# Seeding PSUM with stored products: a recurrence cut into 512 runs of 32 tokens instead of 256 runs of 64

## The chip, the cores and the metric

The kernel runs on one core of a Trainium2 chip. The metric is the device time of one execution in microseconds. Before the change it is 7006.53 us, the median of 3 runs (7005.77 to 7007.88). Engines are called as in the profile: PE is TensorE, with PEld its weight loads, DVE is VectorE, ACT is ScalarE, POOL is GpSimd, and SP issues most of the DMAs.

## What is computed

Four images of 128 channels and 64x64 = 4096 tokens go through a convolution-style attention, a multi-head attention with feed-forward, and at last a recurrent layer. Only the last layer's arithmetic is changed:

```python
def _L1_ffn_ref(x, W, V, gamma, beta):
    Wx = jnp.einsum('bti,hi->bth', x, W)
    flat = Wx.reshape(B * T, H)
    mean = jnp.mean(flat, axis=0)
    var = jnp.var(flat, axis=0)
    Wx = ((flat - mean) * jax.lax.rsqrt(var + BN_EPS) * gamma + beta).reshape(B, T, H)
    def step(yt, wx_t):
        yt = jax.nn.sigmoid(wx_t + yt @ Vt)
        return (yt, yt)
    _, ys = jax.lax.scan(step, y0, jnp.swapaxes(Wx, 0, 1))
...
t = t + _L1_ffn_ref(_ln_t(t), L1_ffn_W, L1_ffn_V, L1_ffn_gamma, L1_ffn_beta)
```

So each token's 128 features are multiplied by W, normalised per feature over all 4x4096 tokens, and then fed one token after another into y = sigmoid(wx + V y), for 4 images side by side. V is orthogonal. The result is added to the token stream. All numbers are fp32.

## The kernel before, in words

**Stages.** Each image goes through a first stage (`first_stage`: the convolution attention of this image, with the feed-forward of the image before it spread in between, lines 1349 to 1395) and a second stage (`second_stage`: its multi-head attention). The last image's feed-forward has a stage of its own (`third_stage`, line 1435). Then come a short stage "fold", the stage "runs" with the recurrence, and the output. A conditional block at the end (line 1602) computes everything again in a slow, sequential way if a check of the result fails.

**Feed-forward.** `feed_forward` (line 1116) is a generator that handles one block of 512 tokens; each `yield` ends a step. In a first stage up to three generators are active and their steps are called from inside the convolution attention (`in_steps`, `meanwhile`), in an order written out by hand for PE, ACT and DVE. In the third stage eight generators run, one started per step, and the framework orders the instructions. At its end a block's normalised tokens are transposed by PE into PSUM (line 1245). `last` (line 1306) then copies them with ACT into SBUF, at once in the order that the recurrence wants (`"p (t c) -> p c t"`, line 1313): for images 0 to 2 into a buffer that SP stores to DRAM (line 1317), for image 3 into `every`. Two steps later `token_products` (line 1252) multiplies them by W on PE into PSUM, and DVE's `bn_stats` (line 1256) reads the product for the statistics; the product itself is thrown away. `hold_every` (line 1459) sets up the tile `every`, 128 channels x 4 images x 4096 tokens, has ACT's queue load images 0 to 2 from DRAM, and GpSimd's queue load W.

**Fold.** `fold_norm` (line 1260) gathers the statistics into `scale` and `shift` per feature, with a power on GpSimd (line 241), scales the rows of W with `scale`, transposes the result on PE and copies it into `WsT`. The normalisation is then W's scaled product plus `shift`.

**Recurrence.** With `C, L = 64, S // 64` (line 1300) an image's 4096 tokens are cut into 64 runs of 64 tokens; all 256 runs of the four images advance together. Every run but an image's first begins with 16 warm-up steps over the last tokens of the run before it (`WARM`, line 1504), so that its state has forgotten where it began. The runs are held in two streams of two images, 128 columns each (`NS`, line 1512). Per step and stream PE does a product with `WsT` of the next step's tokens (`begin`, line 1536, line 1539), a product with V on top of it in PSUM (line 1560), and ACT a sigmoid with `shift` as its bias (line 1567), which overwrites the token in `every`. PE's and ACT's order is written out by hand. There are 16+64 = 80 steps.

**Output.** Sixteen tiles `t2s` of 128 x 1024 hold the stream t2 that the result is added to; SP loads them at the start of the stage (line 1519). After steps 15, 31, 47 and 59 DVE adds the finished tokens of all sixteen tiles (`add_tokens`, line 1543); the last four tokens are added after the loop, tile by tile, with each tile's output DMA behind it, on SP's and ACT's queues in turn (lines 1593 to 1596). DVE also compares each run's end with the warm-up's end of the next run (lines 1580 to 1591); this sets the flag `bad_int` for the conditional block.

Of the kernel before, what the change touches and what calls it, by code (L numbers as in the profile page):

```python
# [10 lines left out]
F32 = mybir.dt.float32  # L11
# [15 lines left out]
def kernel(  # L27
# [32 lines left out]
    P = 128  # L60
# [61 lines left out]
    def half_tile(name):  # L122
        return get("half", name)
# [4 lines left out]
    def one_psum(name):  # L128
        return get("ps_one", name)
# [983 lines left out]
            mirrored(room, *by)  # L1113
        return late[1::2]

    def feed_forward(im, i, t2_rows, last, final):


        n, cols = im["n"], ts(i, IC)
# [123 lines left out]
        yield  # L1243
        yield
        pt = transposed(blocks(u), f"pl{n}_{i}")
        tokens_i = last(n, i, pt)
        yield
        yield
        if n != "r":
            token_products(n, i, tokens_i)  # L1250

    def token_products(n, i, tokens):

        pw = one_psum(f"pwx{n}_{i}")
        nc.tensor.matmul(pw, WT_sb, tokens, start=True, stop=True)
        nc.vector.bn_stats(wx_stats[:, n * NIC + i, :], pw)

    shift = const.tile([P, 1], F32, tag="shift", name="shift")

    def fold_norm(W_sb, WsT):  # L1260

        bmv = once.tile([P, 2], F32, tag="bmv", name="bmv")
        nc.vector.bn_aggr(bmv, wx_stats)
        scale = once.tile([P, 1], F32, tag="scale", name="scale")
        nc.vector.tensor_tensor(scale, rsqrt(bmv[:, 1:2], 1e-5, [P, 1], "bn"), gamma_sb, ALU.mult)
        nc.vector.tensor_tensor(shift, bmv[:, 0:1], scale, ALU.mult)
        nc.vector.tensor_tensor(shift, beta_sb, shift, ALU.subtract)
        Ws = half_tile("Ws")[:, 0:P]
        nc.vector.tensor_scalar(Ws, W_sb, scale, None, ALU.mult)
        pw = one_psum("pws")  # L1270
        nc.tensor.transpose(pw[:, 0:P], Ws, ident)
        nc.vector.tensor_copy(WsT, pw[:, 0:P])
# [24 lines left out]
        }  # L1297


    C, L = 64, S // 64  # L1300

    def feed_forwards(im, final=False):

        n, rows = im["n"], im["rows"]

        def last(n, i, pt):
            cols = ts(i, IC)
            dst = held["every"][:, n, cols] if final else get("fhalf", f"last{n}_{i}")
            if n == "r":
                nc.scalar.copy(dst, pt)  # L1310
            else:

                nc.scalar.copy(
                    dst.rearrange("p (t c) -> p c t", t=L), pt.rearrange("p (c t) -> p c t", t=L)
                )
            if not final:
                nc.sync.dma_start(out=last_dram[rows, cols], in_=dst)
            return dst


        order = [(i + 2 * NTG // NQB) % NTG for i in range(NTG)]
        return [feed_forward(im, i, t2_dram[rows, :], last, final) for i in order]

    def step_first(queue):

# [133 lines left out]
    def hold_every():  # L1459

        pool = ends.enter_context(tc.tile_pool(name="every", bufs=1))
        held["every"] = pool.tile([P, N, S], F32, tag="every", name="every")
        for name in ("W", "WsT"):
            held[name] = pool.tile([P, P], F32, tag=name, name=f"{name}_sb")
        nc.gpsimd.dma_start(out=held["W"], in_=W)
        for n in range(N - 1):
            for i in range(2):
                cols = ts(i, S // 2)
                nc.scalar.dma_start(out=held["every"][:, n, cols], in_=last_dram[ts(n, P), cols])
# [24 lines left out]
    before["close"]()  # L1494


    with stage("fold", half=(HALF, 1), ps_one=(ONE, 1)):
        fold_norm(held["W"], held["WsT"])

    WARM, TOL = 16, 1e-6
    LEAST, MOST = 1e-25, 1e25
    every = held["every"]

    by_run = every.rearrange("p n (i t c) -> p n i t c", t=L, c=IC // L)
# [5 lines left out]
    with stage("runs", t2=((P, 2 * IC), 4 * N), half=(HALF, 2 * NS + 2), ps_one=(ONE, 2 * NS)):  # L1514
# [12 lines left out]
        def tokens_at(k, t):  # L1527
            return by_run[:, ts(k, NN), :, t % L, :]

        def chunks(ap):  # L1530
            return ap.rearrange("p n (i c) -> p n i c", c=IC // L)


        wx = {}

        def begin(k, t):
            wx[k] = one_psum(f"wx{k}_{t + WARM}")[:, 0 : NN * C]
            out_k = wx[k].rearrange("p (n i c) -> p n i c", n=NN, c=IC // L)
            nc.tensor.matmul(
                out_k, held["WsT"], tokens_at(k, t), start=True, stop=t == -WARM, skip_group_check=True  # L1540
            )

        def add_tokens(t0, t1):

            for n, i, t2 in t2s:
                at = t2.rearrange("p (i c t) -> p i t c", i=2, t=L)[:, :, t0:t1]
                nc.vector.tensor_tensor(at, at, by_run[:, n, ts(i, 2), t0:t1], ALU.add)  # L1547


        marks = [0, 16, 32, 48, L - 4, L]  # L1550
        added = {t1: (t0, t1) for t0, t1 in zip(marks, marks[1:-1])}
        with tc.manual_schedule(engines={nc.tensor.engine, nc.scalar.engine}):
            y = [None] * NS
            for k in range(NS):
                begin(k, -WARM)
            for t in range(-WARM, L):
                for k in range(NS):
                    acc = wx[k].rearrange("p (n i c) -> p n i c", n=NN, c=IC // L)
                    if y[k] is not None:
                        nc.tensor.matmul(  # L1560
                            acc, VT_sb, y[k], start=False, stop=True, skip_group_check=True
                        )
                    if t + 1 < L:
                        begin(k, t + 1)
                    w = warm[2 * k + t % 2]
                    y[k] = chunks(w[:, :, 1:]) if t < 0 else tokens_at(k, t)
                    nc.scalar.activation(y[k], acc, AF.Sigmoid, bias=shift)
                    if t == -1:
                        y[k] = chunks(w[:, :, 0:C])
                if t + 1 in added:  # L1570
                    add_tokens(*added[t + 1])
        in_range = small.tile([P, 1], F32, tag="in_range", name="in_range")
        good = half_tile("good")[:, 0 : N * NT]
        inv = inverses.rearrange("p i k -> p (i k)")
        nc.vector.tensor_scalar(good, inv, LEAST, None, ALU.is_ge)
        nc.vector.scalar_tensor_tensor(good, inv, MOST, good, ALU.is_le, ALU.mult)
        nc.vector.tensor_reduce(in_range, good, AX.X, ALU.min)
        ok = half_tile("ok")[:, 0 : N * C].rearrange("p (n c) -> p n c", n=N)
        for k in range(NS):
            nc.vector.tensor_tensor(  # L1580
                chunks(ok[:, ts(k, NN), :]), y[k], chunks(warm[2 * k + 1][:, :, 1:]), ALU.subtract
            )
        nc.vector.tensor_tensor(ok, ok, ok, ALU.mult)
        nc.vector.tensor_scalar(ok, ok, TOL * TOL, None, ALU.is_le)
        nc.vector.tensor_reduce(least, ok, AX.XY, ALU.min)
        nc.vector.tensor_tensor(least, least, in_range, ALU.mult)
        pl = one_psum("pleast")
        nc.tensor.transpose(pl[0:1, 0:P], least, ident)
        nc.vector.tensor_reduce(bad[:, 0:1], pl[0:1, 0:P], AX.X, ALU.min)
        nc.vector.tensor_scalar(bad[:, 1:2], bad[:, 0:1], -1.0, 1.0, ALU.mult, ALU.add)  # L1590
        nc.vector.tensor_copy(bad_int, bad[:, 1:2])

        add_tokens(L - 4, L)
        for n, i, t2 in t2s:
            eng = nc.sync if i % 2 == 0 else nc.scalar
            eng.dma_start(out=out[n][:, ts(i, 2 * IC)], in_=t2)

    ends.close()
    state = const.tile([P, N], F32, tag="state", name="state")
# [2 lines left out]
    with tc.If(any_bad > 0):  # L1602
# [5 lines left out]
        with stage(  # L1608
# [3 lines left out]
            for n in range(N):  # L1612
                nc.sync.dma_start(out=every[:, n, :], in_=last_dram[ts(n, P), :])
                for i in range(NIC):
                    token_products(n, i, every[:, n, ts(i, IC)])
# [96 lines left out]
```

## Time and profile before

| what | us |
|---|---|
| median of 3 runs | 7006.53 |
| the profiled execution's own time | 7005.9 |
| its span, first to last instruction | 7004.2 |
| inside it: `shift` ready / first output DMA issued | 6896.03 / 6978.31 |
| PE busy over the span | 6828.0 (97%) |
| DVE busy over the span | 5934.9 (85%) |
| ACT busy over the span | 5960.0 (85%) |
| POOL busy over the span | 2772.7 (40%) |

The profile is one execution. Its stretches are read by a table of busy times, its single instructions by the timeline: start, length, engine, line, operation, output tile, input tiles, partitions x elements, and how many equal instructions in a row the row stands for; in brackets stands how long the engine was idle ahead of it, and on what it waited. A row of several instructions overlaps with rows of other engines. Groups of instructions give busy time and mean length, and after the second bar the idle time of the engine just before them. Matmul ends are modelled. In the timeline a product in fp32 appears as two passes, each with its own weight load.

### The profile page before, as it was taken

How to read it: one execution, taken by the hardware profiler on the slowest of the kernel's cores; microseconds unless marked ns; L12 is line 12 of the kernel's file. 1: busy time of each engine (PE TensorE's matmuls, PEld its weight loads, DVE VectorE, ACT ScalarE, POOL GpSimd, SP SyncE). 2: the span in 40 equal slices, each digit the busy share in tenths (PEclk: the TensorE clock that was granted, in tenths of full speed). 3: DMA queues.
4: the chain of work that ended last, by engine and by line, in shares of the span. 5: the costliest groups of instructions: out<-in, count | busy, mean ns of one | idle time of the engine just before them, and what ended most of it. 6: DMA issues, size and time to landing. Idle time of an engine off the chain costs nothing. (4 is left out here: it accounts for less than half of the span.)

```text
span 7004.2 us, 224421 instructions
## 1 busy us (share of the span) xinstructions
PE 6828.0 (97%) x92782; PEld 3702.0 (53%) x92782; DVE 5934.9 (85%) x8086; ACT 5960.0 (85%) x11927; POOL 2772.7 (40%) x9893
## 2 busy tenths in 40 slices
PE   8999999999999999999999999999999999999987
PEld 4545555555664555555565555555466555555546
DVE  6688889887888989898787898988878888889884
ACT  4479999996669999999566999999856799999986
POOL 1134444434343444343433443444343444444431
PEclk9999999999999999999999999999999999999998
DMA  1110000000111000000011100000011100000012
GB/s 31 37 41 25 24 27 21 22 10 23 50 54 39 24 21 21 21 21 20 24 47 49 38 21 22 21 25 22 19 31 45 57 22 21 25 29 22 12 62 109
DMA packets 84795, 219.99 MB, mean 31 GB/s; under 512 B 9400, under 2 KB 10304, under 8 KB 82992
## 3 DMA queue, kind: packets, MB, share of 16 engines
q1 hardware_dynamic: 79584, 194.05, 8.3%
q8 instruction: 729, 11.94, 0.7%
q10 hardware_dynamic: 3888, 11.29, 0.4%
q14 instruction: 306, 2.51, 0.1%
q0 software_dynamic: 288, 0.20, 0.0%
HBM read 141.51 MB, written 56.62 MB: 28 GB/s over the span
## 5 line engine op out<-in xcount | busy, mean ns | idle before, releaser
L1021 ACT ACTIVATE e<-s 128x1024 f32<-128x1024 f32 (+1 forms) x3480 | 2952.3, 903 | 114.0 <-PE s L1009 83.9
L826 DVE STREAM_TRANSPOSE t<-e 128x1024 f32<-128x1024 f32 x2240 | 2594.0, 1210 | 77.1 <-ACT e L1021 74.6
L839 PEld LDWEIGHTS misc<-t,mirror 128*32 128x32 f32 x57344 | 1656.9, 110 | 1329.6 <-issue 1271.7
L839 PE MATMUL misc<-t,mirror 128*32 128x128 f32 x57344 | 1968.9, 273 | 20.1 <-DVE later L853 17.2
L1021 ACT ACTIVATE xs<-s 128x1024 f32<-128x1024 f32 (+1 forms) x2152 | 1840.8, 909 | 54.0 <-PE s L1009 41.9
L826 DVE STREAM_TRANSPOSE t<-xs 128x1024 f32<-128x1024 f32 x1344 | 1562.5, 1210 | 42.6 <-ACT xs L1021 41.1
L860 PE MATMUL acc<-e,q_aug 128*32 128x512 f32 x11360 | 1523.7, 609 | 1.0 <-POOL q_aug L742 1.0
L1009 PE MATMUL s<-queries,keys 32*128 32x512 f32 x9216 | 1246.6, 496 | 19.3 <-ACT e L1021 11.4
L902 POOL COPY own<-o 32x36 f32<-32x36 f32 x2048 | 431.1, 211 | 1807.7 <-DVE o L894 1727.7
L514 PE MATMUL acc<-p,asmT 128*128 128x512 f32 x2048 | 945.5, 593 | 1.8 <-DVE e L410 1.6
L860 PE MATMUL acc<-xs,q_aug 128*32 128x512 f32 x7072 | 942.3, 605 | 0.0
L507 ACT ACTIVATE p<-s 128x1024 f32<-128x1024 f32 x512 | 499.6, 1023 | 416.8 <-PE s L503 368.9
L1009 PEld LDWEIGHTS s<-queries,keys 32*128 32x128 f32 x9216 | 488.5, 182 | 600.8 <-issue 295.3
L927 POOL COPY other<-turned 32x64 f32<-32x64 f32 x1904 | 449.5, 236 | 624.4 <-DVE turned L917 545.9
L1021 ACT ACTIVATION_READ_ACCUMULATOR e<-s 128x1 f32 x2880 | 696.6, 242 | 0.0
L796 POOL COPY mirror<-q 32x128 f32<-32x128 f32 x2048 | 597.3, 292 | 199.2 <-PE misc L839 111.3
L503 PE MATMUL s<-hl,e 128*128 128x512 f32 x2048 | 587.9, 428 | 17.9 <-ACT hl L465 11.1
L528 DVE TENSOR_TENSOR total<-total,p 128x1024 f32<-128x1024 f32 x448 | 547.9, 1223 | 25.6 <-ACT p L507 18.1
L514 PEld LDWEIGHTS acc<-p,asmT 128*128 128x128 f32 x2048 | 379.6, 190 | 334.5 <-issue 309.4
L503 PEld LDWEIGHTS s<-hl,e 128*128 128x128 f32 x2048 | 380.8, 189 | 172.7 <-issue 69.5
L1021 ACT ACTIVATION_READ_ACCUMULATOR xs<-s 128x1 f32 x1728 | 422.0, 244 | 0.0
L887 POOL COPY by_token<-by_key 32x4 f32<-32x4 f32 x2016 | 386.9, 192 | 85.1
(261 smaller groups left out, 4559.6 us busy)
## 6 DMA issues: line engine op xcount, KB each, us to landing
keys<-parts_dram SPq DMA_DIRECT2D x256, 256.0 KB
queries<-parts_dram SPq DMA_DIRECT2D x1024, 32.0 KB
fx<-x_dram SPq DMA_DIRECT2D x64, 256.0 KB
x_dram<-x SPq DMA_DIRECT2D x56, 256.0 KB
xs<-in_x_dram SPq DMA_DIRECT2D x16, 512.0 KB
t_dram<-t2T SPq DMA_DIRECT2D x32, 256.0 KB
t2s<-t_dram SPq DMA_DIRECT2D x16, 512.0 KB
hl<-hl SPq DMA_DIRECT2D x28, 256.0 KB
```

What stands on the lines that cost most here:

```text
L503: nc.tensor.matmul(s[:, j, :], stationary, moving, start=y == 0, stop=y == len(parts) - 1)
L507: nc.scalar.activation(p, s, AF.Exp)
L514: nc.tensor.matmul(state["acc", ic], asmT[:, ts(2 * jp + j, P)], p[:, j, :], start=jp == 0 and j == 0, stop=jp == NP - 1 and j == 1,)
L528: nc.vector.tensor_tensor(state[ic], state[ic], p, ALU.add)
L796: nc.gpsimd.tensor_copy(wv[ts(a, 32), s, :, :, ts(a, D)], own[ts(s, 32)])
L826: nc.vector.transpose(group["e"][h][:, k, :], es[h])
L839: nc.tensor.matmul(state["acc"][ts(2 * x + h, 32), :], state["w"][:, QT * (s // 4) + TG * x + s % 4, h, :], state["e"][h][:, :, ds(IC * x ...
L860: nc.tensor.matmul(it["in"]["acc"][ts(2 * h + x, 32), :], it["qa"][:, ds((2 * it["tiles"][x] + h) * V, 32)], it["e"][h][:, ts(x, IC)], sta ...
L902: nc.gpsimd.tensor_copy(own[ts(s, 32), ts(x, 4), h, :], ov[ts(2 * h + x, 32), s, :, 0:V])
L927: copy(to[ts(k, 32), h], tv[ts(2 * x + h, 32), k])
L1009: nc.tensor.matmul(ss[h][:, x, :], keys[unit[x] // QT].bitcast(F32R)[r, ts(unit[x] % QT, P)], queries[b].bitcast(F32R)[r, :], start=True, ...
L1021: nc.scalar.activation(es[h][:, ts(x, IC)] if split else es[h], ss[h][:, x, :] if split else ss[h].rearrange("p x c -> p (x c)"), AF.Exp, ...
```

## The change

The product with W is kept instead of computed twice. In `feed_forward` ACT first copies the transposed tokens as they are; two steps later PE multiplies them by W; one step after that DVE reads the statistics and ACT copies the product, now with the reordering, into `every` or into the buffer that goes to DRAM. The store to DRAM comes after that copy. `every` therefore holds W's products. W is no longer loaded, scaled or transposed, and the stage "fold" is gone.

The runs become 128 per image and 32 tokens long: two streams of 256 columns, 14 warm-up steps, 46 steps in all. Each stream has four PSUM banks of two steps each. A first product with `start=True` covers every bank once. Then DVE writes scale x product + shift for two steps of a stream into a bank ("seed"), PE adds V's product on to it, and ACT's sigmoid has no bias. Eight seeds are written ahead; another follows whenever the second sigmoid of a bank is done. The adds of finished tokens come after steps 9 and 19, two tiles per step, and the last 12 tokens of each tile after the loop, each followed by its output DMA. The check of the result comes after all of these. DVE's order is now written out by hand too.

```diff
@@ feed_forward @@
         pt = transposed(blocks(u), f"pl{n}_{i}")
-        tokens_i = last(n, i, pt)
-        yield
-        yield
-        if n != "r":
-            token_products(n, i, tokens_i)
+        tokens_i = get("fhalf", f"last{n}_{i}")
+        nc.scalar.copy(tokens_i, pt)
+        if n == "r":
+            nc.sync.dma_start(out=last_rows[:, cols], in_=tokens_i)
+            return
+        yield
+        yield
+        pw = token_products(n, i, tokens_i)
+        yield
+        nc.vector.bn_stats(wx_stats[:, n * NIC + i, :], pw)
+        dst = tokens_i if held_wx is None else held_wx[:, cols]
+        nc.scalar.copy(
+            dst.rearrange("p (t c) -> p c t", t=L), pw.rearrange("p (c t) -> p c t", t=L)
+        )
+        if held_wx is None:
+            nc.sync.dma_start(out=last_rows[:, cols], in_=dst)
...
-    C, L = 64, S // 64
+    C, L = 128, S // 128
...
-        for name in ("W", "WsT"):
-            held[name] = pool.tile([P, P], F32, tag=name, name=f"{name}_sb")
-        nc.gpsimd.dma_start(out=held["W"], in_=W)
...
-    with stage("fold", half=(HALF, 1), ps_one=(ONE, 1)):
-        fold_norm(held["W"], held["WsT"])
-    WARM, TOL = 16, 1e-6
+    WARM, TOL = 14, 1e-6
...
+    NB = 8 // NS
+    with stage("runs", t2=((P, 2 * IC), 4 * N), half=(HALF, 2 * NS + 2), ps_one=(ONE, NS * NB)):
...
+        scale = norm_of_products()
+        banks = [[one_psum(f"wx{k}_{j}") for j in range(NB)] for k in range(NS)]
+        for j in range(NB):
+            for k in range(NS):
+                nc.tensor.matmul(
+                    banks[k][j],
+                    ones.bitcast(F32R),
+                    bias_rows[:, 0, :].bitcast(F32R).unsqueeze(1).broadcast_to([P, TG, P]),
+                    start=True,
+                    stop=True,
+                    skip_group_check=True,
+                )
+        def sums_at(k, t):
+            step = t + WARM
+            return banks[k][step // 2 % NB][:, ts(step % 2, NN * C)]
+        def seed(k, t):
+            if t < L:
+                to = banks[k][(t + WARM) // 2 % NB]
+                nc.vector.tensor_scalar(
+                    to.rearrange("p (s a c) -> p a s c", s=2, c=CI),
+                    in_rows[:, ts(k, NN * NIC), ds(t % L, 2), :],
+                    scale,
+                    shift,
+                    ALU.mult,
+                    ALU.add,
+                )
...
-        marks = [0, 16, 32, 48, L - 4, L]
+        marks = [0, 10, 20, L]
+        adds = []
...
+            for t in range(-WARM, 2 * NB - WARM, 2):
+                for k in range(NS):
+                    seed(k, t)
             for t in range(-WARM, L):
                 for k in range(NS):
-                    acc = wx[k].rearrange("p (n i c) -> p n i c", n=NN, c=IC // L)
+                    acc = sums_at(k, t).rearrange("p (n i c) -> p n i c", n=NN, c=CI)
                     if y[k] is not None:
                         nc.tensor.matmul(
                             acc, VT_sb, y[k], start=False, stop=True, skip_group_check=True
                         )
-                    if t + 1 < L:
-                        begin(k, t + 1)
...
-                    nc.scalar.activation(y[k], acc, AF.Sigmoid, bias=shift)
+                    nc.scalar.activation(y[k], acc, AF.Sigmoid)
                     if t == -1:
                         y[k] = chunks(w[:, :, 0:C])
-                if t + 1 in added:
-                    add_tokens(*added[t + 1])
+                    if (t + WARM) % 2:
+                        seed(k, t + 2 * NB - 1)
+                if t + 1 in marks[1:-1]:
+                    adds += [(tile, marks[marks.index(t + 1) - 1], t + 1) for tile in t2s]
+                for _ in range(2):
+                    if adds:
+                        add_tokens(*adds.pop(0))
+            for it in adds:
+                add_tokens(*it)
+            for n, i, t2 in t2s:
+                add_tokens((n, i, t2), *marks[-2:])
+                eng = nc.sync if i % 2 == 0 else nc.scalar
+                eng.dma_start(out=out[n][:, ts(i, 2 * IC)], in_=t2)
```

`norm_of_products` is the first part of `fold_norm`, down to `shift`, and returns `scale`. The slow path keeps W's scaled product.

More of the change, by code (lines that the diff above doesn't have):

```diff
@@ L1114, in attention, with feed_forward @@
         return late[1::2]
-    def feed_forward(im, i, t2_rows, last, final):
+    def feed_forward(im, i, t2_rows, last_rows, held_wx):
         n, cols = im["n"], ts(i, IC)
@@ L1255, in token_products, with norm_of_products @@
         nc.tensor.matmul(pw, WT_sb, tokens, start=True, stop=True)
-        nc.vector.bn_stats(wx_stats[:, n * NIC + i, :], pw)
+        return pw
     shift = const.tile([P, 1], F32, tag="shift", name="shift")
-    def fold_norm(W_sb, WsT):
+    def norm_of_products():
         bmv = once.tile([P, 2], F32, tag="bmv", name="bmv")
@@ L1267, in fold_norm @@
         nc.vector.tensor_tensor(shift, beta_sb, shift, ALU.subtract)
+        return scale
+    def fold_norm(W_sb, WsT):
+        scale = norm_of_products()
         Ws = half_tile("Ws")[:, 0:P]
@@ L1297, in open_image @@
         }
-    C, L = 64, S // 64
+    C, L = 128, S // 128
     def feed_forwards(im, final=False):
         n, rows = im["n"], im["rows"]
[L1306 to L1318, printed above, removed]
         order = [(i + 2 * NTG // NQB) % NTG for i in range(NTG)]
-        return [feed_forward(im, i, t2_dram[rows, :], last, final) for i in order]
+        wx = held["every"][:, n, :] if final else None
+        return [feed_forward(im, i, t2_dram[rows, :], last_dram[rows, :], wx) for i in order]
     def step_first(queue):
@@ L1494 @@
     before["close"]()
-    with stage("fold", half=(HALF, 1), ps_one=(ONE, 1)):
-        fold_norm(held["W"], held["WsT"])
-    WARM, TOL = 16, 1e-6
+    WARM, TOL = 14, 1e-6
     LEAST, MOST = 1e-25, 1e25
     every = held["every"]
-    by_run = every.rearrange("p n (i t c) -> p n i t c", t=L, c=IC // L)
+    CI = IC // L
+    by_run = every.rearrange("p n (i t c) -> p n i t c", t=L, c=CI)
+    in_rows = every.rearrange("p n s -> p (n s)").rearrange("p (a t c) -> p a t c", t=L, c=CI)
     least = const.tile([P, 1], F32, tag="least", name="least")
@@ L1513 @@
     NN = N // NS
-    with stage("runs", t2=((P, 2 * IC), 4 * N), half=(HALF, 2 * NS + 2), ps_one=(ONE, 2 * NS)):
+    NB = 8 // NS
+    with stage("runs", t2=((P, 2 * IC), 4 * N), half=(HALF, 2 * NS + 2), ps_one=(ONE, NS * NB)):
         t2s = []
@@ L1530, in chunks @@
         def chunks(ap):
[L1531 to L1547, printed above, removed]
@@ L1550 @@
-        marks = [0, 16, 32, 48, L - 4, L]
-        added = {t1: (t0, t1) for t0, t1 in zip(marks, marks[1:-1])}
-        with tc.manual_schedule(engines={nc.tensor.engine, nc.scalar.engine}):
+            return ap.rearrange("p n (i c) -> p n i c", c=CI)
+        scale = norm_of_products()
+        banks = [[one_psum(f"wx{k}_{j}") for j in range(NB)] for k in range(NS)]
[9 more added lines that the diff above has]
+                )
@@ L1553, with add_tokens @@
+        def add_tokens(tile, t0, t1):
+            n, i, t2 = tile
+            at = t2.rearrange("p (i c t) -> p i t c", i=2, t=L)[:, :, t0:t1]
+            nc.vector.tensor_tensor(at, at, by_run[:, n, ts(i, 2), t0:t1], ALU.add)
+        marks = [0, 10, 20, L]
+        adds = []
+        with tc.manual_schedule(
+            engines={nc.tensor.engine, nc.scalar.engine, nc.vector.engine}
+        ):
             y = [None] * NS
-            for k in range(NS):
-                begin(k, -WARM)
+            for t in range(-WARM, 2 * NB - WARM, 2):
+                for k in range(NS):
+                    seed(k, t)
@@ L1572 @@
[L1572 to L1596, printed above, removed]
+                    if (t + WARM) % 2:
[5 more added lines that the diff above has]
+                        add_tokens(*adds.pop(0))
@@ new lines @@
+            for it in adds:
[4 more added lines that the diff above has]
+                eng.dma_start(out=out[n][:, ts(i, 2 * IC)], in_=t2)
+            in_range = small.tile([P, 1], F32, tag="in_range", name="in_range")
+            good = half_tile("good")[:, 0 : N * NT]
+            inv = inverses.rearrange("p i k -> p (i k)")
+            nc.vector.tensor_scalar(good, inv, LEAST, None, ALU.is_ge)
@@ new lines @@
+            nc.vector.scalar_tensor_tensor(good, inv, MOST, good, ALU.is_le, ALU.mult)
+            nc.vector.tensor_reduce(in_range, good, AX.X, ALU.min)
+            ok = half_tile("ok")[:, 0 : N * C].rearrange("p (n c) -> p n c", n=N)
+            for k in range(NS):
+                nc.vector.tensor_tensor(
+                    chunks(ok[:, ts(k, NN), :]), y[k], chunks(warm[2 * k + 1][:, :, 1:]), ALU.subtract
+                )
+            nc.vector.tensor_tensor(ok, ok, ok, ALU.mult)
+            nc.vector.tensor_scalar(ok, ok, TOL * TOL, None, ALU.is_le)
@@ L1598 @@
+            nc.vector.tensor_reduce(least, ok, AX.XY, ALU.min)
+            nc.vector.tensor_tensor(least, least, in_range, ALU.mult)
+            pl = banks[0][0]
+            nc.tensor.transpose(pl[0:1, 0:P], least, ident)
+            nc.vector.tensor_reduce(bad[:, 0:1], pl[0:1, 0:P], AX.X, ALU.min)
+            nc.vector.tensor_scalar(bad[:, 1:2], bad[:, 0:1], -1.0, 1.0, ALU.mult, ALU.add)
+            nc.vector.tensor_copy(bad_int, bad[:, 1:2])
     ends.close()
@@ L1614 @@
                 for i in range(NIC):
-                    token_products(n, i, every[:, n, ts(i, IC)])
+                    pw = token_products(n, i, every[:, n, ts(i, IC)])
+                    nc.vector.bn_stats(wx_stats[:, n * NIC + i, :], pw)
             pool, _ = here["big"]
```

## The prediction

> **What bounds the kernel now.** I read the page, then the busy time by stretch over the end of the span, then the timeline there, then the groups of instructions by shape. The change touches the last feed-forward stage, the recurrence and the output tail, some 200 us of 7004; in the attention and convolution stages before it changes only one copy. So the end is what has to be priced.
>
> Busy time by stretch (columns: length, busy us of TensorE, weight loads, VectorE, ScalarE, GpSimd, granted clock, DMA share, GB/s):
>
> ```profile
> 6884.00:6888.00 4.00, 2.08 (x8) 0.96 (x7) 1.70 (x6) 4.00 (x8) 1.47 (x3) 1.00 0.17 66
> 6888.00:6892.00 4.00, 3.06 (x9) 1.42 (x10) 0.85 (x2) 3.98 (x8) 0.00 (x0) 1.00 0.17 66
> 6892.00:6897.00 5.00, 1.24 (x4) 0.24 (x2) 3.30 (x9) 0.86 (x1) 0.58 (x1) 0.85 0.00 0
> 6897.00:6903.00 6.00, 6.00 (x31) 6.00 (x32) 0.00 (x0) 2.53 (x7) 0.00 (x0) 0.56 0.84 288
> 6903.00:6976.00 73.00, 72.11 (x607) 71.77 (x606) 29.43 (x60) 56.37 (x154) 0.00 (x0) 1.00 0.23 93
> 6976.00:7004.00 28.00, 0.37 (x1) 0.08 (x1) 6.23 (x30) 0.00 (x0) 0.00 (x0) 0.52 0.77 303
> ```
>
> Four stages: until 6892 ScalarE is full; to 6897 the norm's statistics are folded; to 6976 TensorE is full (the recurrence); then only DMA works. The timeline gives the anchors and the prices:
>
> ```profile
> 6895.88 0.15 DVE L1267 TENSOR_TENSOR shift<-beta_sb,shift 128x1 f32<-128x1 f32 x1
> ...
> 6897.78 0.80 ACT L1567 ACTIVATE warm<-wx,shift 128x128 f32<-128x128 f32 x2 [4.91 <-PE wx L1539]
> ...
> 6959.94 8.27 DVE L1547 TENSOR_TENSOR t2s<-t2s,every 128x256 f32<-128x256 f32 x16 [6.92 <-ACT every L1567]
> ...
> 6959.99 15.53 ACT L1567 ACTIVATE every<-wx,shift 128x128 f32<-128x128 f32 x33
> ...
> 6971.31 6.40 DVE L1547 TENSOR_TENSOR t2s<-t2s,every 128x192 f32<-128x192 f32 x16 [3.10 <-ACT every L1567]
> ...
> 6978.31 13.58 SPq L1596 DMA_DIRECT2D out_dram<-t2s  x8
> ```
>
> Activations start (15.53-0.37)/32 = 0.474 us apart: 160 of them, from 6897.78 to 6975.52, are 77.7 us, two products (W and V) of TensorE to each. `shift` is ready at 6896.03, the first output DMA goes out at 6978.31 (VectorE was still adding until 6977.7), and the span ends at 7004.2. So: **82.3 us from shift to first output DMA, 25.9 from there to the end.** I price these two, and when shift comes.
>
> **The change part by part.**
>
> *Chain of one stream.* W's product leaves TensorE; 80 double steps become 46. The last product of before runs alone and shows the chain:
>
> ```profile
> 6974.62 0.30 PEld L1560 LDWEIGHTS wx<-every,VT_sb 128*128 128x128 f32 x2 [0.15 <-ACT every L1567]
> 6974.70 0.82 ACT L1567 ACTIVATE every<-wx,shift 128x128 f32<-128x128 f32 x2
> ```
>
> The other stream's activation had ended at 6974.58, 0.05 before the weight load; the last activation starts at 6974.70+0.82-0.37 = 6975.15, so 0.53 from load to activation at 128 columns. A product runs in two passes, which start 0.11 apart here and 0.43 apart at 512 columns (L1255), so 256 columns add 0.11 to each pass: 0.74. The activation: 368 ns at 128 columns with a bias operand; 0.83 ns per element (L398 1115 ns at 1024, L1200 689 at 512), and the bias that falls away is worth 0.09 (L507 without one: 1023 at 1024). So 0.368+0.107-0.09 = 0.385. **A step takes 0.05+0.74+0.385 = 1.175 us**; two streams then need 0.86 of TensorE and 0.77 of ScalarE, so neither binds. 46 of them are 54 us where 77.7 were.
>
> *VectorE.* It gets a seed of 512 elements per stream and two steps (eight at the start, then one per bank set free; each waits for the bank's second activation, with adds queued behind it, and TensorE waits for it in turn), and adds of 320 elements, two a step, after steps 9 and 19. The adds: 8.27/16 = 0.52 at 256 and 0.40 at 192, or 1.8 ns per element, against 1.2 for unstrided 512 (L1233, 0.60 apart). The stride of 64 elements becomes 32, still strided: **0.63 for 320, 0.75 for 384**; bounds 0.50 (unstrided rate) and 0.75. No row shows VectorE writing such a tensor into PSUM. Neighbours:
>
> ```profile
> 34.21 0.75 DVE L339 SCALAR_TENSOR_TENSOR asmT<-za,aa_sb,ya 128x512 f32<-128x512 f32 x1 [1.80 <-ACT za L338]
> ...
> 34.88 1.00 DVE L378 TENSOR_SCALAR q<-xs,gm,r_g 128x512 f32<-128x512 f32 x2
> ```
>
> L378 is the same operation, SBUF to SBUF, 0.46 apart. But the Trainium skill (VectorE: DVE Perf Modes, What auto-detection actually checks) gives the two-port double rate only where source and destination are in SBUF. So I take L339's rate, 0.67 apart with one per-partition scalar, plus 0.06 for the second (L378 544 ns against L246's 421 with none): **0.72 a seed**; bounds 0.46 and 0.82. By L378 the sixteen seeds below cost 7.4 us, by the rule 11.5.
>
> *Sum.* Shift to first seed 0.72, to the first activation 0.76. Step 9 is the 24th: 0.76+23x1.175+0.385+0.6 (second stream, half a period later) = 28.8. TensorE restarts at half clock (0.56 in 6897-6903, where a pair took 1.71); the eight opening products on the banks warm it partly: between 0 and 1.9 us lost, I take 1.2. So 30.0. From there VectorE has 16 seeds (11.5) and 32 adds (20.3) and doesn't idle: until step 19, 11.75 us on, it has 17.3 us of work. It ends at 61.8, later than the chain (55.8 if never held). Lag reaches some 6 us, near the lead that four banks give (6 steps, 7 us), so products begin to wait for seeds; that moves the chain's end, not VectorE's. First final add and issue 0.85: **62.7 against 82.3, 19.6 saved.**
>
> A second rule speaks against the edit: the skill's PSUM — Partial Sum Buffer (Summary: rules for kernel authors) lets only zero be a seed, and its section The four PSUM rules sends other seeds through TensorE. That would be the old W product at 256 columns: 4x0.43 = 1.71 a pair, 78.7 us, nothing gained. The same section says that a product adds to what VectorE wrote where an earlier product had marked the element, as the opening products do. No row of this trace shows it; the instructions and their time are the same whether it adds or not, so I take the time of the change's form.
>
> *Last feed-forward stage.* The copy of 1.09 us per block stays, moved behind the product, and a plain one joins it:
>
> ```profile
> L1313 ACT COPY every<-pl 128x512 f32<-128x512 f32 x8 | 8.5, 1092 | 0.0
> L1239 ACT COPY t2T<-pt 128x512 f32<-128x512 f32 x7 | 3.9, 577 | 0.0
> ```
>
> ScalarE is full here (0.0 idle before them), so eight plain copies at 0.47 apart cost 3.8 on the path, less one or two of the long ones (0.86 apart) that now fall behind the last product, beside the statistics: **+2.4 us**, between +2 and +4. W's scaling, transpose and copy (6895.69 to 6896.89) come after shift and were in the 82.3. The last long copy and the 1.28 us table load lie beside the 3 us of statistics; without that cover they would cost up to 1.
>
> *Earlier stages.* 24 plain copies of 0.59 and 24 moved ones go into convolution stages where, from 1700 to 2050, TensorE is busy 348.5 of 350 us and ScalarE 219: 0, up to +3 in all. The moved copy now waits for W's product, with the next Exp queued behind it and TensorE's score products waiting on that; but it is issued a step after the product, so the product is done. Its PSUM tile is held a step longer, which is the +3. The 24 stores to DRAM go out some four steps later on SP's queue, with loads queued behind; the readers (6784) come 1300 us after the last. GpSimd's load of W (0.67 us) had 110 us to spare. 0.
>
> *Tail.* The same 8.4 MB at 400 GB/s. Final adds of 0.75 feed 512 KB each, faster than the 1.3 us DMA needs. The flag's chain now follows all adds: 15x0.75+3.3 = 14.6 after the first DMA instead of 2.6, then 1.2 of loading and the 6 us that SP waited after its branch: 22, before the DMAs' 23.8. 0, with 2 us to spare at most; up to +2.
>
> Sum: -19.6+2.4 = -17.2. The profiled execution took 7005.9 (span 7004.2); this gives 6988.7, and the median of 7006.5 gives 6989.3: **6989**.
>
> **The rivals.**
> *VectorE keeps up* (seeds nearer 0.5, adds nearer 0.5): the chain sets the end, 55.8+0.8 = 56.6; 25.7 saved, less 2.4: 6983. For it: L378. Against: the PSUM output.
> *VectorE and ScalarE dearer* (0.82, 0.75, last stage +3.5): 30.0+13.1+24.0+0.9 = 68; 14.3-3.5 = 10.8 saved: 6996. Tail or convolution stages giving back 2 to 6 us end here too.
> *The clock* (slower): TensorE goes from 99% to about 73% busy with waits in every step; if it were granted half clock, a pair takes 1.71 to 2.1 us (loads hidden or not). 46 pairs are 79 to 97: 7009 to 7025. From 1.69 a pair it is slower than before. Against it: 6884-6888, half busy at clock 1.00.
> *It doesn't do what it says*: 14 warm-up steps fail the end test and the fallback computes all again, doubling the time; a sigmoid's slope of at most 1/4 and an orthogonal V leave 4^-14, far under 1e-6.
>
> **How the numbers follow.** VectorE sets the end 0.58 (6985 to 6993), keeps up 0.14, dearer 0.22, clock 0.04, else 0.02. The range, 6981 to 6998, takes in the first three with their bounds. About 0.2% (14 us, 6992.5) is what a measurement can tell from no change: faster 0.55+0.14+0.04 = 0.73, same 0.23, slower 0.04.
>
> **What would show it.** Seeds 0.72 and adds 0.63 apart; activations 1.17 per pair until step 9, then waits of TensorE on VectorE; VectorE without a gap from step 9 to the last add; clock 1.00; shift 2.4 later; 25.9 from first output DMA to the end. I am wrong if pairs take 1.3 before any add is queued, if VectorE idles in the second half, or if the end waits for the flag.

## The result, and the profile after

The changed kernel takes 6993.82 us (median of 18 runs, 6985.99 to 6996.79) where the kernel before takes 7006.55 (18 runs, 6999.91 to 7008.2): a ratio of 0.9982, with a 95% interval from 0.9974 to 0.9989. That is 12.7 us less, somewhere between 7.7 and 18.2. I had said 6989, 4.8 lower. I had also put 0.73 on a gain of more than 14 us, which I took for the least that can be told from no change; the median falls just short of that mark, and yet the interval leaves no change out. The profiled execution of the changed kernel took 6996.23 us, its span is 6994.4.

I read the profile after in the order of before. First the busy time by stretch (columns as before: length, TensorE, weight loads, VectorE, ScalarE, GpSimd, granted clock, DMA share, GB/s):

```profile
6896.00:6900.00 4.00, 2.74 (x10) 1.17 (x8) 1.40 (x2) 4.00 (x8) 0.00 (x0) 1.00 0.91 219
6900.00:6904.60 4.60, 2.81 (x10) 1.27 (x8) 3.16 (x8) 3.33 (x4) 0.58 (x1) 1.00 0.77 243
6904.60:6910.00 5.40, 4.79 (x13) 2.96 (x14) 5.40 (x9) 2.69 (x7) 0.00 (x0) 0.68 0.97 361
6910.00:6932.00 22.00, 21.25 (x77) 11.03 (x75) 15.92 (x22) 14.58 (x38) 0.00 (x0) 1.00 0.49 196
6932.00:6962.00 30.00, 27.04 (x94) 13.68 (x92) 29.20 (x45) 17.98 (x47) 0.00 (x0) 1.00 0.00 1
6962.00:6966.00 4.00, 0.00 (x0) 0.00 (x0) 4.00 (x8) 0.04 (x1) 0.00 (x0) 1.00 0.00 0
6966.00:6994.00 28.00, 0.37 (x1) 0.08 (x1) 13.90 (x26) 0.00 (x0) 0.00 (x0) 0.51 0.78 303
```

VectorE is full from 6932 on (29.20 of 30, then 4.00 of 4.00 while TensorE and ScalarE have nothing left). TensorE starts the recurrence at a granted clock of 0.68 and has 1.00 in the stretches behind it, although its queue has gaps. The timeline has the anchors:

```profile
6903.49 0.16 DVE L1278 TENSOR_TENSOR shift<-beta_sb,shift 128x1 f32<-128x1 f32 x1
6903.79 10.09 DVE L1552 TENSOR_SCALAR wx<-every,scale,shift 128x512 f32<-128x512 f32 x14
6904.64 0.39 ACT L1586 ACTIVATE warm<-wx 128x256 f32<-128x256 f32 x1 [1.12 <-DVE wx L1552]
...
6910.04 0.82 ACT L1586 ACTIVATE warm<-wx 128x256 f32<-128x256 f32 x2 [0.36 <-PE wx L1581]
6910.48 0.73 PEld L1581 LDWEIGHTS wx<-warm,VT_sb 128*128 128x128 f32 x4 [0.44 <-ACT warm L1586]
6911.21 0.82 ACT L1586 ACTIVATE warm<-wx 128x256 f32<-128x256 f32 x2 [0.35 <-PE wx L1581]
...
6959.06 2.56 PE L1581 MATMUL wx<-every,VT_sb 128*128 128x256 f32 x8 [1.35 <-DVE wx L1552]
6959.54 16.46 DVE L1565 TENSOR_TENSOR t2s<-t2s,every 128x320 f32<-128x320 f32 x24
```

A pair of activations every 1.17 us (6910.04 to 6911.21); near the end TensorE waits 1.35 us for a seed. Now VectorE's groups in the second half (busy, then mean ns of one):

```profile
L1565 DVE TENSOR_TENSOR t2s<-t2s,every 128x320 f32<-128x320 f32 x32 | 20.4, 707 | 0.0
L1552 DVE TENSOR_SCALAR wx<-every,scale,shift 128x512 f32<-128x512 f32 x16 | 12.1, 804 | 0.8 <-ACT every L1586 0.8
```

From start to start these are 0.62 us an add and 0.714 a seed (they overlap by about 0.09, as before). Last the end of the chain view, before and then after:

```profile
6981.31 0.92 DVE t2s L1547 x5
```

```profile
6980.01 0.29 DVE bad L1619
6980.30 0.02 issue
6980.32 0.15 DVE bad L1620
6980.47 0.02 issue
6980.49 0.14 DVE bad_int L1621
```

Before, the chain that ended last closes with the adds that feed the output transfers. After, it closes with the flag of the convergence check.

The profiles of all kernels of this study can be laid over each other at four places. The convolution stages count from TensorE's first wait of over 1 us in them (the time ahead of it varies by over 1 us between stages of one and the same kernel) to their last exponential (line 507), as a mean of the three that hold a feed-forward; "to shift" counts from the last exponential of attention 3. The attention stages are left out: they are the same code in all of these kernels and scatter by up to 3 us from profile to profile.

| kernel | convolution stage | to shift | shift to first output transfer | from there to end | sum against before | median against its before |
|---|---|---|---|---|---|---|
| before | 418.02 | 135.36 | 82.28 | 25.87 | | |
| after | 418.74 | 136.98 | 61.63 | 29.16 | -13.6 | -12.7 |
| e1_ff_only | 418.77 | 137.10 | 81.75 | 25.86 | +3.4 | +3.1 |
| e2_rec_only | 418.00 | 134.80 | 60.52 | 29.18 | -19.1 | -18.9 |
| e3_w_on_pe | 418.00 | 135.29 | 83.56 | 25.93 | +1.2 | +1.1 |
| e4_pool_adds | 418.75 | 136.94 | 56.69 | 29.27 | -18.4 | -18.9 |
| e5_flag_early | 418.74 | 137.05 | 61.59 | 27.32 | -15.4 | -15.0 |
| e6_copy_vec | 420.47 | 133.72 | 60.52 | 29.29 | -12.6 | -10.8 |
| e7_copy_later | 418.80 | 135.23 | 60.60 | 29.38 | -16.0 | -14.3 |
| e8_copy_first | 416.97 | 136.01 | 61.92 | 29.12 | -19.6 | -18.2 |
| e9_together | 416.88 | 135.71 | 58.27 | 27.15 | -25.8 | -24.3 |

The sum is three convolution stages plus the three other columns. It meets the measured medians within 1.8 us in all ten cases, so to within that the change is in these four places. The columns are read from one execution of each kernel, and the ratios below have intervals of some 4 to 10 us to either side, so a difference of 1 or 2 us between two variants rests on these columns. Where kernels share their code, the convolution stage and the tail repeat within 0.1 to 0.3 us. "To shift" repeats less well: from 134.80 to 135.36 with the old feed-forward (before, e2, e3), and from 135.23 to 136.01 in e7, e8 and e9. Against before, the four places give for the changed kernel +2.2, +1.6, -20.7 and +3.3. I had +0, +2.4, -19.6 and 0.

### The profile page after: what moved, and what is told of

The parts are those of the page before. It is cut to its first block, busy times and chain, and to the rows that moved or that the text cites. A ratio compares the mean times of both kernels' runs of the same rounds, so it can differ in the third digit from the quotient of the medians.

```text
span 6994.4 us, 223485 instructions
## 1 busy us (share of the span) xinstructions
PE 6811.6 (97%) x92333; PEld 3656.1 (52%) x92333; DVE 5967.4 (85%) x8098; ACT 5952.9 (85%) x11891; POOL 2772.9 (40%) x9892
## 5 line engine op out<-in xcount | busy, mean ns | idle before, releaser
L839 PE MATMUL misc<-t,mirror 128*32 128x128 f32 x57344 | 1969.0, 273 | 18.4 <-DVE later L853 15.5
```

The costliest lines, as they stand in the source:

```text
L839: nc.tensor.matmul(state["acc"][ts(2 * x + h, 32), :], state["w"][:, QT * (s // 4) + TG * x + s % 4, h, :], state["e"][h][:, :, ds(IC * x ...
```

## The experiments

**e1_ff_only and e2_rec_only: one half each.** e1 is the kernel before with the new `feed_forward`; e2 is the changed kernel with the old one. e2 leaves W's product out of the recurrence, which it feeds with the scaled tokens, so it is a test of time alone.

```
e1   -        tokens_i = last(n, i, pt)
     +        tokens_i = get("fhalf", f"last{n}_{i}")
     +        nc.scalar.copy(tokens_i, pt)
     ...      (product, statistics and long copy as in the changed kernel)
     -        fold_norm(held["W"], held["WsT"])
     +        fold_norm(ident, held["WsT"])
e2   the reverse in the changed kernel's feed_forward
```

> The kernel before with the changed feed-forward alone: the extra plain copy, the product, the long copy behind it, products stored and kept. The recurrence stays at 64 runs of 64 tokens with W on TensorE; so that it still computes the reference, the fold starts from the identity in place of W. Theory (ScalarE's second copy costs at the end of the last feed-forward stage and in the convolution stages): shift comes 1.6 to 2.4 us later behind the last exponential of attention 3, each convolution stage is 0.5 to 1.5 us longer with one gap of about 1.6 us on TensorE that the kernel before does not have, shift to first output transfer stays at 82.3 and the tail at 25.9; the time is 2 to 6 us above before. Rival (only the last stage pays, the rest of what the changed kernel's profile shows upstream is scatter): no new gap in the convolution stages, and about 2 us above before.

> The changed kernel with the feed-forward of before: one long copy, no plain copy, so tokens and not products are kept, and the recurrence is fed with scaled tokens where the reference has scaled products (the W product is left out of the recurrence's sums; it is still made for the norm). Recurrence and tail are those of the changed kernel. Theory: last exponential to shift back at 135.4 us, convolution stages as in before, shift to first output 61.6, tail 29.2; 20.7 less and 3.3 more, so 17 us under before, 4 to 5 under the changed kernel. Rival (the upstream part is scatter): 15 us under before, within 2 of the changed kernel.

Measured: e1 7009.75 against 7006.69, ratio 1.0006 (0.9997 to 1.0014); e2 6987.83, ratio 0.9972 (0.9961 to 0.9982). e1's median lies within its uncertainty, but its places are plain: 137.10 to shift, and in each convolution stage the 0.7 us and the new gap. e2 has neither. So the feed-forward gives back 3 to 4 us, and the recurrence with its tail gains 17 to 19. From shift to the first output transfer, e2 is 1.1 us faster (60.52) than the changed kernel. The granted clock goes with it: in the 5 us from 1.2 us behind shift, first the changed kernel, then e2:

```profile
6904.86:6909.86 5.00, 4.65 (x13) 2.82 (x14) 5.00 (x8) 2.47 (x7) 0.00 (x0) 0.66 0.97 365
```

```profile
6900.03:6905.03 5.00, 4.52 (x16) 2.40 (x17) 5.00 (x8) 3.25 (x9) 0.00 (x0) 1.00 1.03 415
```

At 0.66 the first pairs come 1.68, 1.71 and 1.27 us apart, at 1.00 they come 1.24, 1.17 and 1.17 apart: 1.1 us. Over the same 5 us the profiles of e4, e5, e8 and e9 show 0.66 too, those of e6 and e7 show 1.00. Why one kernel wakes at full clock and the other doesn't, with the same opening products, these runs don't settle.

**e3_w_on_pe: fewer steps, W's product kept on TensorE.**

```
-    C, L = 64, S // 64
+    C, L = 128, S // 128
-    WARM, TOL = 16, 1e-6
+    WARM, TOL = 14, 1e-6
-        marks = [0, 16, 32, 48, L - 4, L]
+        marks = [0, 8, 16, 24, L - 4, L]
```

> The kernel before at 128 runs of 32 tokens an image (256 columns a product, 14 warming steps), with W's product still on TensorE in every step and the sums added at 8, 16, 24, 28 and 32: the rule's way of starting a sum. Theory (at 256 columns a step pair is then four products on TensorE): 1.71 us a pair, 46 pairs 78.7, shift to first output about 80 against 82.3, so the time is within 3 us of before. Rival (the halved step count alone is the gain, TensorE's W product hides under the activations): a pair at 1.17 to 1.3, shift to first output near 60, and the time 20 us under before.

Measured: 7007.83, ratio 1.0002 (0.9993 to 1.001). The activations in mid recurrence:

```profile
6912.72 0.47 ACT L1567 ACTIVATE warm<-wx,shift 128x256 f32<-128x256 f32 x1 [0.39 <-PE wx L1560]
6913.58 0.48 ACT L1567 ACTIVATE warm<-wx,shift 128x256 f32<-128x256 f32 x1 [0.39 <-PE wx L1560]
6914.44 0.47 ACT L1567 ACTIVATE warm<-wx,shift 128x256 f32<-128x256 f32 x1 [0.39 <-PE wx L1560]
```

One every 0.86, a pair in 1.73, each waiting for TensorE. Half as many steps of twice the width gain nothing as long as TensorE makes both products; the gain comes when W's product leaves the step. The other half alone, 80 steps with seeds, was not run. An estimate from the lone product of before (0.05 of hand-off, 0.53 from load to activation, 0.28 of activation without a bias) is 80 x 0.86 = 69 us of pairs if VectorE kept up, against 77.7 before and 54 for 46 pairs of 1.17: most of the gain would then need both. Of the 3.5 us over my "about 80", 2.4 are the first two pairs, 3.41 and 2.46 apart.

**e4_pool_adds: lighten VectorE.**

```
-                for _ in range(2):
+                for by in (nc.gpsimd, nc.vector):
                     if adds:
-                        add_tokens(*adds.pop(0))
+                        add_tokens(*adds.pop(0), by)
```

> The changed kernel with every second of the 32 adds that lie inside the recurrence on GpSimd, which is idle there; 16 stay on VectorE. Theory (VectorE's queue sets the end of the recurrence): VectorE loses 16 x 0.62 = 10 us of work, the pairs no longer wait for seeds (the changed kernel lost 2.4 us in three such waits), the chain of products and activations sets the end: last activation at shift + 56.0, first output transfer at shift + 57.2 in place of 61.6, so 4.4 us under the changed kernel, 17 under before. Rival A (the chain already sets the end): shift to first output stays at 61.6. Rival B (GpSimd's adds slow VectorE's own, or take so long that the last adds wait for them): VectorE's adds rise over 0.62 apart or the first output transfer waits for GpSimd, 62 or more.

Measured: 6986.52 against 7005.46, ratio 0.9974 (0.9964 to 0.9984). Shift to first output falls by 4.9 us, to 56.69, the last activation comes at shift + 56.0, and after the third pair every pair is within 0.01 of 1.17: the three waits of the changed kernel (pairs of 1.34, 1.82 and 2.73) are gone. Near the end of e4:

```profile
6948.97 0.84 ACT L1586 ACTIVATE every<-wx 128x256 f32<-128x256 f32 x2 [0.34 <-PE wx L1581]
...
6950.15 0.84 ACT L1586 ACTIVATE every<-wx 128x256 f32<-128x256 f32 x2 [0.34 <-PE wx L1581]
```

So VectorE's queue was the bound. GpSimd's help has a price, which the groups between 6927 and 6951 show:

```profile
L1565 POOL TENSOR_TENSOR t2s<-t2s,every 128x320 f32<-128x320 f32 x16 | 19.1, 1238 | 32.4 <-ACT every L1586 32.4
L1565 DVE TENSOR_TENSOR t2s<-t2s,every 128x320 f32<-128x320 f32 x12 | 13.2, 1171 | 0.0
```

VectorE's adds take 1171 ns beside GpSimd's, where they took 707 alone. Of rival B that half is true; VectorE had the room.

**e5_flag_early: the check out of the end of VectorE's queue.**

```
-                nc.vector.tensor_tensor(
+                nc.gpsimd.tensor_tensor(
                     chunks(ok[:, ts(k, NN), :]), y[k], chunks(warm[2 * k + 1][:, :, 1:]), ALU.subtract
...
+            for at, (n, i, t2) in enumerate(t2s):
+                check(at)
+                add_tokens((n, i, t2), *marks[-2:])
```

> The changed kernel with the convergence check off the end of VectorE's queue: its differences, squares and comparison on GpSimd, its range test at step -8 of the recurrence, and VectorE's five remaining short steps behind the 8th and the 10th of the 16 last adds. Theory (the end waits for the check's flag and the branch behind it): the branch on SP comes when its last output transfer is issued, near last-add time, about 2.7 us earlier than in the changed kernel; the output transfers end at the same time; first output to end falls from 29.2 to 26 or 27, 2 to 3 us under the changed kernel. Rival (output transfers or the fetch of instructions behind them set the end, whatever the time of the branch): first output to end stays at 29, or gets longer by the 1.4 us that VectorE's adds are pushed back.

Measured: 6990.43, ratio 0.998 (0.9972 to 0.9987); first output to end 27.32, 1.8 less, a little short of the 2 to 3 that I expected, and not by the way I expected. SP's branch comes 17.1 us behind the first transfer, no earlier than the changed kernel's 16.9, because VectorE stood still for 3.8 us and its last adds with SP's last transfer came later:

```profile
6967.86 0.69 DVE L1616 TENSOR_REDUCE least<-ok 128x1 f32<-128x512 f32 x1 [3.77 <-POOL ok L1611]
```

What came earlier is the branch of three other engines: VectorE's, TensorE's and GpSimd's 12.8, 12.6 and 12.5 us behind the first transfer (ScalarE's came later, at 18.5), where all five engines of the changed kernel branch within 0.4 us (6981.83 to 6982.19). Behind its branch SP then needs 6.3 us to its next instruction instead of 7.4, and 1.6 instead of 2.6 at a second stop. That the earlier branches shorten these two is not shown.

**e6_copy_vec, e7_copy_later, e8_copy_first: the two copies.** e6 puts the plain copy on VectorE; e7 has a `yield` ahead of the long copy; e8 turns long copy and statistics round in the convolution stages and keeps e7's `yield` in the last one.

```
e6   -        nc.scalar.copy(tokens_i, pt)
     +        nc.vector.tensor_copy(tokens_i, pt)
e7            nc.vector.bn_stats(wx_stats[:, n * NIC + i, :], pw)
     +        yield
e8   +        if held_wx is not None:
     +            nc.vector.bn_stats(wx_stats[:, n * NIC + i, :], pw)
     +            yield
              nc.scalar.copy(...)
              if held_wx is None:
     +            nc.vector.bn_stats(wx_stats[:, n * NIC + i, :], pw)
```

> The changed kernel with the plain copy of the transposed tokens on VectorE in place of ScalarE, in the convolution stages and in the last feed-forward stage. If ScalarE's load as a whole is the cost: last exponential to shift falls by 1.5 to 2 us (to about 135.3) and the gap of 1.6 us on TensorE in each convolution stage goes. If in the convolution stages it is the place of the long copy, which waits for the product with exponentials queued behind it: the last stage gains, and the gap of 1.6 us stays. Rival (VectorE, 85% busy over the span, is as dear): last exponential to shift stays at 137 or grows.

> The changed kernel with the long copy handed to ScalarE one turn of the interleaving later (one more yield ahead of it). Theory (in each convolution stage one long copy waits 3.7 us for its product at the head of ScalarE's queue, between a table load and the next, with two exponentials behind it, and TensorE waits 1.6 us for these): the gap of 1.6 us is gone, each convolution stage is 0.8 us shorter (417.9 from the end of its first gap to its last exponential, where the changed kernel has 418.7), 2 to 3 us in all; the last feed-forward stage unchanged, 137.0. Rival (the sum of the copies' time is the cost, wherever they stand): another gap takes its place and the stages stay at 418.7.

> The changed kernel with the long copy ahead of the statistics in the convolution stages, and one turn behind the statistics in the last feed-forward stage (where that turn alone gave 1.7 us). Theory (the long copy waits for VectorE's statistics of the same product, which stand behind six products for the next stage on VectorE's queue, and the exponentials wait behind the copy): the copy runs about 3 us earlier, right behind the sine, the 1.6 us gap on TensorE is gone or under 0.6, each convolution stage goes from 418.7 to about 418.0, the last stage has 135.2; 3.5 us under the changed kernel. Rival (the copy's own 1.1 us is the cost, wherever it stands before the exponentials): the gap stays over 1.2.

Measured, against 7005.46 as for e4 and e5: e6 6994.67, ratio 0.9986 (0.9979 to 0.9992); e7 6991.16, 0.998 (0.9973 to 0.9988); e8 6985.53 against 7003.71, 0.9973 (0.9964 to 0.9983). What TensorE waits for in the first of the three convolution stages (us in total, times, longest), in before, after, e6 and e8:

```profile
PE s L503 <- ACT p L507: 1.7, 2, 1.1
```

```profile
PE s L503 <- ACT p L507: 3.3, 3, 1.6
PE pq L291 <- DVE q L675: 1.9, 1, 1.9
```

```profile
PE s L503 <- ACT p L507: 3.3, 3, 1.6
PE pq L291 <- DVE q L675: 2.5, 1, 2.5
```

```profile
PE s L503 <- ACT p L507: 1.7, 2, 1.1
```

e6 unloads ScalarE and the third wait, of 1.6 us, stays; the wait for VectorE grows as well, from 1.9 to 2.5, and the stage is 1.7 us longer than in the changed kernel. So ScalarE's load isn't the cause of that wait. ScalarE's queue near the gap names it, first the changed kernel, then e8:

```profile
2080.28 0.72 ACT L255 ACTIVATE r<-r,half_pi 128x512 f32<-128x512 f32 x1
2084.74 1.08 ACT L1257 COPY last<-pwx 128x512 f32<-128x512 f32 x1 [3.73 <-DVE wx_stats L1255]
2085.84 1.28 ACT L507 ACT_TABLE_LOAD   x1
2087.14 1.94 ACT L507 ACTIVATE p<-s 128x1024 f32<-128x1024 f32 x2
```

```profile
2080.72 0.72 ACT L255 ACTIVATE r<-r,half_pi 128x512 f32<-128x512 f32 x1
2081.35 1.03 ACT L1259 COPY last<-pwx 128x512 f32<-128x512 f32 x1
2082.40 1.28 ACT L507 ACT_TABLE_LOAD   x1
2083.69 1.94 ACT L507 ACTIVATE p<-s 128x1024 f32<-128x1024 f32 x2
```

The long copy stood 3.73 us at the head of ScalarE's queue, released by VectorE's statistics of the same product, with the table load and two exponentials behind it. VectorE's queue in that time, in the changed kernel:

```profile
2081.04 0.28 DVE L673 TENSOR_TENSOR q<-r 128x64 f32<-128x64 f32 x1 [0.98 <-ACT r L255]
2081.35 2.75 DVE L675 TENSOR_TENSOR q<-q,r 128x64 f32<-128x64 f32 x6
2084.02 0.69 DVE L1255 BATCH_NORM_STATS2 wx_stats<-pwx 128x6 f32<-128x512 f32 x1
```

The statistics stand behind the steps for the next attention, and the copy starts at 2084.74, when they end. Both only read the product. The Trainium skill says why one waits for the other all the same (PSUM — Partial Sum Buffer, PSUM bank collisions raise a hardware error): two engines may not be at one PSUM bank at once, two readers included, and the compiler puts a dependency between them. The trace agrees: the statistics end at 2084.71 and the copy starts 0.03 later. With the copy ahead of the statistics it follows the sine at once, the exponentials start 2.97 us behind the sine's start instead of 6.86, and the stage is 1.8 us shorter than in the changed kernel. That it is also 1.1 shorter than before I have not taken apart. e7 missed in these stages: its copy came one turn later but still ahead of the same exponentials (3.73 us of waiting again). Unlooked for, it gained 1.7 us in the last feed-forward stage, where the framework sets the order. e8 has the same lines there and gains 1.0, where I expected 1.7, so that turn is worth about 1 to 1.7; e6, with the plain copy off ScalarE, gains 3.3.

**e9_together.** e4's adds, one mark more (8, 16, 24 in place of 10 and 20), the range test at step -8, and e8's copies.

```
-        marks = [0, 10, 20, L]
+        marks = [0, 8, 16, 24, L]
```

> The changed kernel with every second inner add on GpSimd, the sums added at 8, 16, 24 and 32 (so that a last add has 256 elements in place of 384), the range test at step -8, the check otherwise behind the last adds on VectorE as before, and the long copy moved as in the run beside this one. Theory: last stage 135.2 (-1.7), convolution stages -0.7 each (-2), shift to first output 55.4 (-6.2: no cold first pairs, no waits for seeds), flag at 11.5 and SP's branch at about 14 us behind the first output transfer in place of 16.9, so the end at 26 to 27 behind it in place of 29.2 (-2.5): 12 us under the changed kernel, 25 under before. Rival for the tail (the fetch behind the branch ends when the output transfers do): end at 29 still, and 10 under. Rival for the recurrence (with 24 adds each, GpSimd at 1.0 to 1.4 us an add falls behind the pairs of 1.17): first output transfer 60 or more behind shift.

Measured: 6979.43 against 7003.71, ratio 0.9965 (0.9952 to 0.9979), 24.3 us under before, where the changed kernel has 0.9982 (0.9974 to 0.9989). The tail is 27.15: SP branches 13.0 us behind the first transfer, and its next instruction 7.0 later then finds transfers still on their way. Shift to first output is 58.27 where I had 55.4: the clock was low again in the first pairs (1.24, 2.04, 1.66, so 1.4 us), and the last inner adds ran 1.2 us past the last activation. The pairs themselves stay at 1.17.

## Why the prediction was right, and where it was not

- *One step pair in 1.175 us.* Measured 1.17, and term by term: 0.06 of hand-off, 0.73 from load to activation and 0.38 of activation, where I had 0.05, 0.74 and 0.385. e4 shows the chain bare.
- *A seed 0.72, an add 0.63 for 320 elements and 0.75 for 384, VectorE sets the end at 61.8.* Measured 0.714, 0.622, 0.714, and 60.8. Had the double rate that needs both ends in SBUF applied here too, a seed would have come near L378's 0.46; a seed into PSUM costs 0.714. I took its rate from another operation, so the closeness is in part luck. The seed also writes its elements in rows of 16 in another order than it reads them, and no run tells the two apart. e4 takes 10 us of adds away and the end moves by 4.9, to the chain: 56.7, which is the rival "VectorE keeps up" (56.6), made true by hand.
- *Cold clock 1.2 us.* 1.1, by the first pairs of e2, e6 and e7, which have clock 1.00.
- *Seeds through TensorE gain nothing (78.7 us).* e3: 46 pairs of 1.73, 79.6, and no gain in time.
- *Last feed-forward stage +2.4.* Measured +1.6 in the changed kernel and +1.7 in e1 against before, and up to 2.2 against e2, which has the old code and is at 134.80. The plain copies are there, with no idle time ahead of them, and two long ones start after the last product has started, about as I had it. An order of the copies that is about 1 us cheaper was to be had (e7, e8).

```profile
L1247 ACT COPY last<-pl 128x512 f32<-128x512 f32 x8 | 5.0, 629 | 0.0
```

- *Earlier stages 0, up to +3 in all.* Measured +2.2. The step that failed: "it is issued a step after the product, so the product is done". The product was done (it had ended at 2077.1); the copy waited for VectorE's statistics of the same product, which stood behind seven of VectorE's instructions for the next attention. I looked for the wait at the operand and not at the other reader of the same PSUM tile. e8, which changes only the order of the two readers there, takes the wait of 1.6 us away.
- *Tail 0, up to +2, flag chain 22 against the transfers' 23.8.* Measured +3.3; I had written that I would be wrong if the end waited for the flag, and there it does. My terms: flag 14.6 (measured 15.4), loading and branch 1.2 (1.5), 6 us behind the branch (7.4), sum 22 (24.3). Then come 0.4 of semaphore checks, a second stop of 2.6 us that I had no term for, and 1.8 of closing. Neither stop is a wait for an output transfer: the semaphore checked behind the first was complete at 14.9, the one behind the second at 24.3, three microseconds before its check at 27.35. The transfers ended at 23.8 as predicted:

```profile
6985.30:6988.30 3.00, 0.00 (x0) 0.00 (x0) 0.00 (x0) 0.00 (x0) 0.00 (x0) 0.50 0.67 214
6988.30:6991.30 3.00, 0.00 (x0) 0.00 (x0) 0.00 (x0) 0.00 (x0) 0.00 (x0) 0.50 0.11 31
6991.30:6994.40 3.10, 0.00 (x0) 0.00 (x0) 0.00 (x0) 0.00 (x0) 0.00 (x0) 0.50 0.01 3
```

From 6989 on almost nothing moves, and the end comes 5 us later. e5 and e9, in which some engines branch earlier, get back 1.8 and 2.0 of the 3.3; the rest I did not take apart.

So the recurrence went as predicted, 1.1 us better, and the two places that I priced at nothing because something covered them gave back 5.5 us together. With the last feed-forward stage 0.8 better, the terms miss by 3.6 in sum. The distance between 6989 and 6993.8 is 4.8, and the rest lies in the 0.9 by which the table misses the median and in rounding. That the number came this close is in part luck: two misses of 5.5 us stood against 1.9 us of gains.

## What to carry to other kernels

When work leaves the engine that bounds a stage, size the engine that takes it over by its own queue, seed by seed and add by add: here it became the bound, and moving half of its inner adds to an idle engine took another 4.9 us off the recurrence. Here the second reader of a PSUM tile waited for the first one, so a moved copy is priced by what stands in the other engine's queue, not only by its operand. A check that closes with a branch is covered by output transfers only if what follows the branch is counted too.

## What I had not expected of the hardware

- The first instruction behind a branch comes 6 to 7.4 us later while output transfers run (before 6.0, after 7.4, e5 6.3, e9 7.0). The trace has packets of the instruction queues among the output packets in that time; that the engine waits for these, and they behind the output, is my reading, and no run here separates it.
- A GpSimd subtraction of 256 elements lasted 8.6 us in e5 while VectorE ran adds back to back, and ended 0.4 us after VectorE's queue had come to a stand; the next of the same shape took 0.62 (spans on GpSimd are rough in this profile). The two together, and then the rest:

```profile
6955.93 9.19 POOL L1607 TENSOR_TENSOR ok<-every,warm 128x256 f32<-128x256 f32 x2 [59.03 <-ACT every L1586]
6965.20 1.04 POOL L1610 TENSOR_TENSOR ok<-ok 128x512 f32<-128x512 f32 x1
```

With e4's rows (a VectorE add 1171 ns beside GpSimd's, 707 alone) this fits what the Trainium skill states (SBUF — State Buffer, SBUF: two separate sides): a VectorE instruction with two inputs in SBUF and a GpSimd instruction that reads SBUF need the same pair of ports; whichever starts first has it for its whole length, and the other is blocked. In e5 the subtraction did not end until VectorE paused; in e4 and e9 both engines' adds went on side by side, each longer. What decides between the two was not tried.
- TensorE kept clock 1.00 from 6910 to the end of the recurrence, with 27.04 us of work in 30 in the second half and waits in every step.
